# Reordering GpSimd's queue, one chunk's scores and one product in a two-layer attention kernel

## The chip, the cores and the metric

The kernel runs on one core of a Trainium2 chip. The metric is the device time of one launch in microseconds (us); the time before is the median of three runs.

## The reference

The input x holds 8 samples of 128 channels by 48 x 48 positions, float32: 2304 tokens of 128 channels each. What is computed, cut to what matters (group norm, leaky ReLU and layer norm as usual; `q`, `k`, `v` are projections of the normalized input with its position table; `_to_tokens` and `_from_tokens` only transpose):

```python
    # layer 0
    attn = jnp.einsum('bkn,bkm->bnm', q, k) / jnp.sqrt(jnp.float32(Kdim))
    attn_masked = attn * mask + (1.0 - mask) * -10000.0       # mask: lower triangle
    attn_masked = jax.nn.softmax(attn_masked, axis=-1) * mask
    x = x + jnp.einsum('bnm,bvm->bvn', attn_masked, v)
    # layer 1, on tokens
    t = _to_tokens(x)
    n = _ln_t(t)
    t = t + jnp.einsum('bnm,bmd->bnd', softmax(jnp.einsum('bnd,bmd->bnm', n, n)), n)
    # a recurrence over the 2304 tokens, with batch statistics of Wx
    t = t + _L1_ffn_ref(_ln_t(t), W, V, gamma, beta)
    x = _from_tokens(t, x)
```

In the second attention queries and keys are the same tensor, so its matrix of scores is symmetric.

## The kernel before, in words

**Tiles.** A sample's 2304 tokens are 6 chunks of 384 (`QC`), each of 3 blocks of 128. Samples, chunks and blocks are counted from 0. Partition size is 128 throughout; everything is float32. In names such as s_1_2_6, the numbers are sample, chunk and block.

**Per sample, about 204 us, there are two parts.** `Causal` does the masked attention of layer 0. For chunk j and block m up to the diagonal: scores on TensorE (PE, L1032), exponential on ScalarE (ACT, L1034), for blocks on the diagonal a multiplication with a triangle on GpSimd (POOL, L1037, the "mask"), then the product with the values on PE (L1043). VectorE (DVE) adds up the sums (L1054, L1058). When a chunk is complete, `Causal.after` starts a chain of steps: sums, residual (L1105), inverse root on POOL (`rooted`, L943), normalization on DVE (`normed`, L948). Then, for chunks 0 to 3, the normalized tokens are turned through memory; for chunks 4 and 5 `back` transposes them on PE (tile tb, L953) and ACT copies them into xh (L1129), and `shifted` adds 1 to the token-major copy xhT (POOL, L1124) and takes 1 off the residual t1t (POOL, L1125).

`Full` does the second attention. It uses the symmetry: only blocks at or right of the diagonal are scored ("direct": score L1294, exponential L1296, product L1316). The transposes of these are used for the other half. For a block of a later chunk n, DVE transposes 32 x 32 squares into a tile t (L1261); three of these fill it, `store` writes it to DRAM tile e_j_n with four DMAs of SyncE (SP, L1212), and `load` reads it back as tile g_i_j (SP, L1204; three buffers) for the "turned" products of chunk j (L1304). Blocks in a chunk's own triangle are "mirrored": DVE (L1229), out to DRAM (`out_of`, POOL, tile m, L1242), back in with four DMAs (`back_in`, POOL, tile gm, L1246), products at L1312, which are the chunk's last items. When a chunk is complete, `Full.after` starts its chain: a copy of the result (L1336), transposes (of_t, L953), residual and moments on DVE, root on POOL (L1368), a transpose of the roots (L1373), `spread` (SP: roots and turned result to DRAM, L1379, L1382), `fetch` (SP: t2x at L1386 and scale at L1388), `product` (the FFN weights times t2x on PE, tile wx, L1394; an ACT copy in `keep`; DVE at L1395 and L1396) and `stored`.

At the end comes the recurrence, which the change doesn't touch.

**What sets the order.** One list, `stream`, holds all items (one score with its product) of all samples. An item's score is issued three items ahead of its product (`LAG`). The first three items of the next sample's `Causal` are woven into the last six of a sample's stream. `Full.items()` orders a chunk's direct and turned items by a fraction, (k + 0.5) / count, for each kind. Everything else, such as the chains of the `after` methods and the next sample's projections (`project`: PE L895 and L898, tiles pj, read by DVE at L902 and L903), is issued between items by a planner, `Stream`. It keeps an estimate of the time (`now`) and of when each engine is free. A step is (function, PE cost, list of engine costs), and sets when the next step of its chain is due; a cost with an empty engine name is a plain delay. After each item `tick` runs up to two steps that are due:

```python
    def run(self, chain):
        work, cost, ops = chain.steps.popleft()
        ...
        end = self.spend(cost, chain.at) if cost else max(self.now, chain.at)
        chain.at = self.then(end, ops)
        work()
    ...
    def finish(self, chain):
        while chain.steps:
            self.run(chain)
        self.now = max(self.now, chain.at)
```

So `finish` issues all that is left of a chain at once and moves the planner's time to its end. Engines execute what is issued to them in this order; semaphores guard the data. `Full.begin` of chunk 0 finishes the chain of the chunk of `Causal` whose tokens it needs, so the transposes tb of chunk 5 are issued right ahead of the score of block 15. Prefetching g tiles (`prefetch`) is tried at every item of `Full`: loads first, then stores that are due.

Of the kernel before, what the change touches and what calls it, by code (L numbers as in the profile page):

```python
# [604 lines left out]
def fast_path(ctx: ExitStack, tc: tile.TileContext, x, pe, w_ffn, out, x_tok, w_qkv, w_pos, v_t, gamma_beta, flag):  # L605
    nc = tc.nc
# [7 lines left out]
    NQ = N // QC  # L614
# [52 lines left out]
    with ExitStack() as actx:  # L667
# [16 lines left out]
        def psum_s(name):  # L684
            return ps_s.tile([P, CH], F32, tag="s", name=name)
# [6 lines left out]
        def chunk_tile(tag, name, holder=None, steps=0, bufs=2):  # L692

            if holder is not None:
                before = holders.setdefault(tag, deque([({}, 0)] * bufs))
                old, n = before.popleft()
                before.append((holder, steps))
                if "chain" in old:
                    st.advance(old["chain"], n)
            return (work if bufs == 2 else work1).tile([P, QC], F32, tag=tag, name=name)  # L700
# [85 lines left out]
        st = Stream()  # L786
# [74 lines left out]
        def following(b, n=None):  # L861

            if n is not None:
                whole[b] = n
            n = whole.get(b, -1) + 1
            if 0 < n < NQ and n <= allowed.get(b, EARLY) and (b, n) not in projected:
                project(b, n)
# [55 lines left out]
        def bounds(b):  # L923

            qk = small2.tile([P, 2], F32, tag="qk", name=f"qk_{b}")
            nc.vector.tensor_reduce(qk, largest[b], AX.X, ALU.max)
            nc.vector.tensor_mul(bound[:, b : b + 1], qk[:, 0:1], qk[:, 1:2])
# [18 lines left out]
        def normalize(dst, y, mv, rs):  # L946
            for g in range(QB):
                nc.vector.tensor_scalar(dst[:, ts(g, P)], y[:, ts(g, P)], mv[:, g, 0:1], rs[:, g : g + 1], ALU.subtract, ALU.mult)  # L948
# [49 lines left out]
        def listed(chunks):  # L998
            return [(j, w, i == 0, i == len(ws) - 1) for j, ws in enumerate(chunks) for i, w in enumerate(ws)]

        t1_tok, x_hat, normed_chunks = {}, {}, {}

        class Causal:
# [5 lines left out]
            @staticmethod  # L1009
            def items():  # L1010

                chunks = []
                for j in range(NQ):
                    others, own = list(range(QB * j)), list(range(QB * j, QB * (j + 1)))
                    chunks.append(others[:QB] + own + others[QB:])
                return listed(chunks)
# [4 lines left out]

            def begin(self, j, m, first):
                b = self.b
                if first:
                    st.finish(projected[b, j])
                    allowed[b] = j + EARLY
                    following(b)
                    if j == NQ - 1:
                        bounds(b)
                off = self.offset(j, m)  # L1030
                s = psum_s(f"s_{b}_{j}_{m}")
                nc.tensor.matmul(s[:, off:QC], keys[b][:, ts(m, P)], queries[b, j][:, off:], start=True, stop=True)  # L1032
                p = pp.tile([P, QC], F32, tag="p", name=f"p_{b}_{j}_{m}")
                nc.scalar.activation(p[:, off:], s[:, off:QC], AF.Exp, scale=SCALE)  # L1034
                ops = [("ACT", 0.16 + (QC - off) * 0.00085)]
                if m >= QB * j:
                    nc.gpsimd.tensor_mul(p[:, off : off + P], p[:, off : off + P], triu)  # L1037
                    ops.append(("POOL", 0.5))
                return p, st.then(st.spend((QC - off) * US), ops)
# [21 lines left out]
            def after(self, j, o):  # L1061
                b = self.b
# [5 lines left out]
                if far:  # L1068
                    ot = turn_result(o, f"c_{b}_{j}", c, False)
                    at = st.then(st.now, [("DVE", 0.57)])  # L1070
                    through = token_major(c, ot, f"c_{b}_{j}", "toc", 5)
                else:
                    o_sb = chunk_tile("o", f"oc_{b}_{j}", c, 3)
                    nc.scalar.copy(by_block(o_sb), o[:, :QC].rearrange("p (a g r) -> p a g r", a=R, g=QB))
                    at = st.then(st.now, [("ACT", 0.5)])
# [38 lines left out]
                def normed():  # L1114
# [4 lines left out]
                    c["y"] = x_hat[b][0][:, QB * j : QB * (j + 1), :].rearrange("p g c -> p (g c)")  # L1119
                    normalize(c["y"], t1_tok[b, j], c["mv"], c["rs"])  # L1120

                def shifted():

                    nc.gpsimd.tensor_scalar_add(c["y"], c["y"], 1.0)  # L1124
                    nc.gpsimd.tensor_scalar_add(t1_tok[b, j], t1_tok[b, j], -1.0)  # L1125

                def back():
                    tp = transposed(c["y"], f"tb_{b}_{j}")
# [15 lines left out]
                def get():  # L1144
# [5 lines left out]
                ways = [  # L1150
                    (turn_normed, 0.0, [("DVE", 0.57)]),
                    (shifted, 0.0, [("POOL", 1.2)]),
                    (put, 0.0, [("", 4.0)]),
                    (get, 0.0, [("", 4.0)]),
# [13 lines left out]
        class Full:  # L1168
# [12 lines left out]
            @staticmethod  # L1181
            def items():
                chunks = []
                for j in range(NQ):
                    ahead = [("direct", QB * n + g) for n in range(j, NQ) for g in range(QB)]
                    turn = [("turned", i, g) for i in range(j) for g in range(QB)]
                    both = [((k + 0.5) / len(ahead), w) for k, w in enumerate(ahead)]
                    both += [((k + 0.5) / len(turn), w) for k, w in enumerate(turn)]
                    order_of = [w for _, w in sorted(both, key=lambda e: e[0])]
                    for own in ahead[QB - 2 :: -1]:  # L1190
                        order_of.remove(own)
                        order_of.insert(0, own)
                    chunks.append(order_of + [("mirrored", g) for g in range(1, QB)])
                return listed(chunks)
# [28 lines left out]
            def mirror(self, j, g, p, ready):  # L1223

                b, left = self.b, QB - 1 - g
                if g == 0:
                    self.tm = chunk_tile("tm", f"tm_{b}_{j}", bufs=1).rearrange("p (b q r) -> p b q r", b=R, q=QB)
                first = g * (QB - 1)
                nc.vector.transpose(  # L1229
                    self.tm[:, :, first : first + left, :].rearrange("p b q r -> p q b r"),  # L1230
                    p[:, (g + 1) * P :].rearrange("p (q b r) -> p q b r", q=left, b=R),
                )
                at = st.then(ready, [("DVE", 0.17 + left * 0.13)])
                if g < QB - 2:
                    return
                gm = chunk_tile("gm", f"gm_{b}_{j}", bufs=1).rearrange("p (a q r) -> p a q r", a=R, q=QB)
                self.gm = gm
                d = dpool.tile([P, R, QB * SQ], F32, tag=f"m_{j % 2}", name=f"m_{b}_{j}")
                tm = self.tm

                def out_of():
                    nc.gpsimd.dma_start(d, tm.rearrange("p b q r -> p b (q r)"))  # L1242

                def back_in():
                    for r in range(R):
                        nc.gpsimd.dma_start(  # L1246
                            gm[ts(r, SQ)].rearrange("c a q r -> c a (q r)"), d.rearrange("(a c) b f -> b c a f", a=R)[r]
                        )

                self.moved = st.add([(out_of, 0.0, [("POOL", 1.2), ("", 3.0)]), (back_in, 0.0, [("POOL", 5.0), ("", 3.0)])], at + 0.6 - st.now)  # L1250

            def turned(self, j, m, p, ready):

# [70 lines left out]
            def after(self, j, o):  # L1324
                b = self.b
# [4 lines left out]
                if far:  # L1330
                    ot = turn_result(o, f"f_{b}_{j}", c, True)
                    at = st.then(st.now, [("DVE", 0.57)])
                    through = token_major(c, ot, f"f_{b}_{j}", "tof", 3)
                else:
                    o_sb = chunk_tile("o", f"of_{b}_{j}", c, 1)
                    nc.scalar.copy(o_sb, o[:, :QC])  # L1336
                    at = st.then(st.now, [("ACT", 0.5)])
# [106 lines left out]
                if last:  # L1444
                    steps = [
                        (keep_last, 0.35, [("ACT", 0.85)]),
                        (normed, 0.0, [("DVE", 1.1)]),
                        (back, 0.35, [("ACT", 0.5)]),
                        (statistics, QC * US, [("DVE", 0.55), ("ACT", 0.85)]),
                    ]  # L1450
                else:
                    steps = [
                        (turn_root, 0.0, [("DVE", 0.15)]),
                        (spread, 0.0, [("", 13.0)]),
                        (fetch, 0.0, [("", 9.0)]),
                        (product, QC * US, [("DVE", 1.0)]),
                        (stored, 0.0, [("ACT", 0.85)]),
                    ]
# [31 lines left out]
        LAG = 3  # L1490
        stream = []
        for b in range(B):
            part, items = Causal(b), Causal.items()
            if b:

                for k in range(QB):
                    stream.insert(len(stream) - 2 * QB + k + 1, (part, *items[k]))
                items = items[QB:]
            stream += [(part, *i) for i in items]
            part = Full(b)  # L1500
            stream += [(part, *i) for i in part.items()]
        ready, o = {}, {}
        for n in range(len(stream) + LAG):
            if n < len(stream):
                part, j, what, first, last = stream[n]
# [5 lines left out]
            if n >= LAG:  # L1511
                part, j, what, first, last = stream[n - LAG]
# [200 lines left out]
```

## Time and profile before

| what | value |
|---|---|
| median of three runs | 1737.05 us (1737.0 to 1739.15) |
| the profiled run's own time | 1735.51 us |
| its span, first to last instruction | 1733.7 us |
| granted TensorE clock | 0.996 |
| score or product of 384 columns on PE (L1316, four matmuls for two) | 1.29 us for two |
| mask on POOL (L1037), mean | 471 ns |
| issue of one gm load on POOL (L1246), mean | 562 ns |
| root on POOL (L943; L1368), mean | 995 ns; 881 ns |
| shift on POOL (L1124), mean | 1296 ns |
| gm load, issue to landing, least / median / most | 2.1 / 3.3 / 6.9 us |

In the profile, a line of the timeline gives the start in us, the duration in us, the engine, the line of the kernel, the operation and its output and inputs; "x4" means four instructions one after the other, and brackets hold how long the engine had stood idle and what ended that. SPq is SyncE's queue, which issues DMAs. A line of the waits gives who waited for what, the total, the times and the longest.

### The profile page before, as it was taken

The page shows a single profiled execution, that of the slowest core. Times are in us where ns is not written, and L with a number is a line of the kernel's source. Part 1 is how long each engine was busy: PE and PEld are TensorE (multiplying, and loading weights), DVE is VectorE, ACT ScalarE, POOL GpSimd, SP SyncE. Part 2 cuts the span into 40 slices and gives each one's busy share as a digit, 9 for nine tenths or more (in the row PEclk, how much of TensorE's full clock was granted, in tenths as well). Part 3 has the DMA queues.
Part 4 walks back from the last instruction along what each step waited for, and adds up shares of the span by engine and source line. Part 5 has one row for each costly group of instructions (what it writes and reads, how often), then busy time and mean ns, then how long its engine had stood idle before and what let it go on. Part 6 is the DMA issues. An engine that isn't in the chain of part 4 may idle for free.

```text
span 1733.7 us, 22462 instructions
## 1 busy us (share of the span) xinstructions
PE 1692.1 (98%) x6243; PEld 1083.3 (62%) x6243; DVE 1205.0 (70%) x3291; ACT 684.4 (39%) x1300; POOL 445.2 (26%) x637
## 2 busy tenths in 40 slices
PE   9999999999999999999999999999999999999986
PEld 6666666666666666666666666666666666666665
DVE  5875578656886478855786567864688556884467
ACT  3344334443344423443344433443334432444345
POOL 1232122311233122321214112332213212242116
PEclk9999999999999999999999999999999999999998
DMA  3336764578445874468635675447843687247868
GB/s 121 106 89 201 229 192 114 128 204 244 135 108 143 226 237 124 88 193 236 200 105 123 188 233 151 124 121 224 254 132 78 165 233 226 64 98 200 222 235 221
DMA packets 316586, 291.13 MB, mean 168 GB/s; under 512 B 195777, under 2 KB 280674, under 8 KB 315940
## 3 DMA queue, kind: packets, MB, share of 16 engines
q1 hardware_dynamic: 306284, 267.71, 54.9%
q0 software_dynamic: 9936, 21.51, 4.5%
q8 instruction: 51, 0.84, 0.2%
q14 instruction: 83, 0.68, 0.1%
q10 hardware_dynamic: 232, 0.40, 0.1%
HBM read 163.61 MB, written 125.90 MB: 167 GB/s over the span
## 4 chain that ended last, share of the span: by engine, by line
PE 89%; DMA 5%; DVE 2%; SPq 1%; POOL 1%; issue 1%; ACT 1%; DVEq 0%; POOLq 0%; ACTq 0%
PE s L1032 17%; PE o L1043 17%; PE s L1294 15%; PE o L1316 15%; PE o L1304 11%; PE pj L895 3%; DMA g<-e 2%; DMA t2x<-t_d 2%; PE z L1626 2%; PE o L1312 2%; PE pj L898 2%; PE wx L1394 2%; SPq L1212 1%; POOL gm L1246 1%; PE of_t L953 1%
## 5 line engine op out<-in xcount | busy, mean ns | idle before, releaser
L1296 ACT ACTIVATE p<-s,shift 128x384 f32<-128x384 f32 (+2 forms) x504 | 274.8, 551 | 552.2 <-PE s L1294 482.7
L1034 ACT ACTIVATE p<-s 128x384 f32<-128x384 f32 (+2 forms) x504 | 231.1, 461 | 410.7 <-PE s L1032 359.7
L1294 PE MATMUL s<-xh 128*128 128x384 f32 (+2 forms) x1008 | 379.8, 458 | 4.5 <-ACT xh L1129 4.5
L1043 PE MATMUL o<-p,vT 128*128 128x384 f32 (+2 forms) x1008 | 377.7, 456 | 4.7 <-POOL p L1037 4.7
L1032 PE MATMUL s<-q,k 128*128 128x384 f32 (+2 forms) x1008 | 380.6, 459 | 0.1
L1316 PE MATMUL o<-p,xhT 128*128 128x384 f32 (+2 forms) x1008 | 367.6, 456 | 0.0
L1304 PE MATMUL o<-g,xhT 128*128 128x384 f32 x720 | 276.2, 487 | 6.1 <-DMA g<-e 6.1
L1261 DVE STREAM_TRANSPOSE t<-p 128x384 f32<-128x384 f32 x360 | 183.8, 549 | 139.2 <-DMA e<-t 90.3
L1316 PEld LDWEIGHTS o<-p,xhT 128*128 128x128 f32 x1008 | 189.2, 190 | 118.8 <-ACT p L1296 0.3
L1043 PEld LDWEIGHTS o<-p,vT 128*128 128x128 f32 x1008 | 186.7, 190 | 115.8 <-POOL p L1037 9.0
L1294 PEld LDWEIGHTS s<-xh 128*128 128x128 f32 x1008 | 184.2, 190 | 110.2 <-ACT xh L1129 6.5
L1032 PEld LDWEIGHTS s<-q,k 128*128 128x128 f32 x1008 | 182.3, 190 | 98.3 <-issue 2.2
L1058 DVE TENSOR_TENSOR acc<-acc,p 128x384 f32<-128x384 f32 (+2 forms) x408 | 209.2, 513 | 22.5 <-ACT p L1034 1.2
L1304 PEld LDWEIGHTS o<-g,xhT 128*128 128x128 f32 x720 | 131.5, 190 | 84.2 <-DMA g<-e 8.8
L1037 POOL TENSOR_TENSOR p<-p,triu 128x128 f32<-128x128 f32 x144 | 67.2, 471 | 437.1 <-ACT p L1034 436.9
L1246 POOL DMA_DIRECT2D gm<-m x192 | 106.9, 562 | 67.4 <-PE pj L895 30.6
L1368 POOL TENSOR_TENSOR roots<-ve_f,mhalf 128x3 f32<-128x3 f32 x48 | 42.3, 881 | 252.2 <-DVE ve_f L937 252.0
L1124 POOL TENSOR_SCALAR xhT<-xhT 128x384 f32<-128x384 f32 x48 | 62.2, 1296 | 106.7 <-DVE yt L1133 56.8
L1242 POOL DMA_DIRECT2D m<-tm x48 | 29.0, 605 | 208.3 <-DVE tm L1229 207.8
L1395 DVE TENSOR_TENSOR scale<-wx,scale 128x384 f32<-128x384 f32 x46 | 25.6, 556 | 80.2 <-PE wx L1394 72.4
L895 PE MATMUL pj<-xn,wT 128*128 128x384 f32 x192 | 77.9, 488 | 1.5 <-DVE xn L888 1.5
L902 DVE TENSOR_TENSOR q<-pj,pb 128x384 f32<-128x384 f32 x48 | 26.7, 556 | 68.9 <-PE pj L895 68.9
(250 smaller groups left out, 1695.7 us busy)
## 6 DMA issues: line engine op xcount, KB each, us to landing
e<-t SPq DMA_DIRECT2D x480, 144.0 KB
g<-e SPq DMA_DIRECT2D x120, 576.0 KB
pb<-posb_d SPq DMA_DIRECT2D x42, 576.0 KB
t1t<-in_x_tok_dram SPq DMA_DIRECT2D x48, 192.0 KB
m<-tm POOLq DMA_DIRECT2D x48, 192.0 KB, 4.4
gm<-m POOLq DMA_DIRECT2D x192, 48.0 KB, 3.3
t_d<-tt SPq DMA_DIRECT2D x184, 48.0 KB
t2x<-t_d SPq DMA_DIRECT2D x46, 192.0 KB
```

What stands on the lines that cost most here:

```text
L895: nc.tensor.matmul(ps[:, :QC], wT[:, j, :], xn, start=True, stop=True)
L1032: nc.tensor.matmul(s[:, off:QC], keys[b][:, ts(m, P)], queries[b, j][:, off:], start=True, stop=True)
L1034: nc.scalar.activation(p[:, off:], s[:, off:QC], AF.Exp, scale=SCALE)
L1037: nc.gpsimd.tensor_mul(p[:, off : off + P], p[:, off : off + P], triu)
L1043: nc.tensor.matmul(o[:, off:QC], vals[b][:, ts(m, P)], p[:, off:], start=first, stop=last)
L1058: nc.vector.tensor_add(a[:, off:], a[:, off:], p[:, off:])
L1246: nc.gpsimd.dma_start(gm[ts(r, SQ)].rearrange("c a q r -> c a (q r)"), d.rearrange("(a c) b f -> b c a f", a=R)[r])
L1261: nc.vector.transpose(t[:, :, :, g, :].rearrange("p b j r -> p j b r"), p.rearrange("p (j b r) -> p j b r", j=QB, b=R))
L1294: nc.tensor.matmul(s[:, off:QC], xh[:, ts(m, P)], xh[:, j * QC + off : (j + 1) * QC], start=True, stop=True)
L1296: nc.scalar.activation(p[:, off:], s[:, off:QC], AF.Exp, bias=shift)
L1304: nc.tensor.matmul(out_ap, xhT[:, QB * i + g, :], p, start=first, stop=last)
L1316: nc.tensor.matmul(o[:, off:QC], xhT[:, what[1], :], p[:, off:], start=first, stop=last)
```

## The change

Four edits, all to the order of issue:

- At the first item of each sample but the first, the chain that moves the previous sample's last mirrored blocks (m out, gm in) is finished (`st.finish(self.behind.moved)`). `behind` is the previous sample's `Full`.
- In `Causal.after`, the second shift (-1 on t1t) of chunk 4 becomes a step of its own, due 12 us later; for chunk 0 of `Full`, `back_in` is due 12 and not 3 us after `out_of`.
- In `Full.items()`, the places of chunk 4's direct items are multiplied by 0.6, so that they come earlier among the turned ones.
- In `Full.after`, `product` is due 12 and not 9 us after `fetch`.

```diff
@@ Causal.begin
                 b = self.b
+                if first and b and j == 0:
+                    st.finish(self.behind.moved)
                 if first:
                     st.finish(projected[b, j])
@@ Causal.after
+                def lowered():
+                    nc.gpsimd.tensor_scalar_add(t1_tok[b, j], t1_tok[b, j], -1.0)
+
                 def shifted():
 
                     nc.gpsimd.tensor_scalar_add(c["y"], c["y"], 1.0)
-                    nc.gpsimd.tensor_scalar_add(t1_tok[b, j], t1_tok[b, j], -1.0)
+                    if j == NQ - 2:
+                        st.add([(lowered, 0.0, [("POOL", 1.2)])], 12.0)
+                    else:
+                        lowered()
@@ Full.items
-                    both = [((k + 0.5) / len(ahead), w) for k, w in enumerate(ahead)]
+                    both = [((k + 0.5) / len(ahead) * (0.6 if j == NQ - 2 else 1.0), w) for k, w in enumerate(ahead)]
@@ Full.mirror
-                self.moved = st.add([(out_of, 0.0, [("POOL", 1.2), ("", 3.0)]), (back_in, 0.0, [("POOL", 5.0), ("", 3.0)])], at + 0.6 - st.now)
+                self.moved = st.add([(out_of, 0.0, [("POOL", 1.2), ("", 12.0 if j == 0 else 3.0)]), (back_in, 0.0, [("POOL", 5.0), ("", 3.0)])], at + 0.6 - st.now)
@@ Full.after
-                        (fetch, 0.0, [("", 9.0)]),
+                        (fetch, 0.0, [("", 12.0)]),
                         (product, QC * US, [("DVE", 1.0)]),
@@ the stream
         for b in range(B):
+            behind = stream[-1][0] if b else None
             part, items = Causal(b), Causal.items()
+            part.behind = behind
```

## Prediction

> **What bounds the kernel now.** I read the engines' busy time on the page first, then TensorE's waits, then the stretch of time around each kind of wait.
>
> ```profile
> PE 1692.1 (98%) x6243; PEld 1083.3 (62%) x6243; DVE 1205.0 (70%) x3291; ACT 684.4 (39%) x1300; POOL 445.2 (26%) x637
> ```
>
> PE is busy for 1692.1 of 1733.7 us, and no other engine comes near. The built programs hold the same instructions on every engine before and after; only their order differs. So PE's busy time stays, and the change can move nothing but the 41.6 us in which PE stands idle. TensorE's waits, the largest first, say what those are (line, what ended the wait: us in total, times, longest):
>
> ```profile
> PE o L1304 <- DMA g<-e: 6.1, 6, 2.4
> PE o L1043 <- POOL p L1037: 4.7, 7, 0.7
> PE s L1294 <- ACT xh L1129: 4.5, 8, 0.6
> PE wx L1394 <- DMA t2x<-t_d: 3.8, 5, 1.2
> ...
> PE o L1312 <- DMA gm<-m: 1.6, 1, 1.6
> ```
>
> The first four make 19.1 us, and come at the same place in most of the eight samples (counted from 0). The mask wait is read from GpSimd's timeline at the first change of sample (start, duration):
>
> ```profile
> 228.43 0.87 POOL L1368 TENSOR_TENSOR roots<-ve_f,mhalf 128x3 f32<-128x3 f32 x1 [6.42 <-DVE ve_f L937]
> 232.88 0.46 POOL L1037 TENSOR_TENSOR p<-p,triu 128x128 f32<-128x128 f32 x1 [3.58 <-ACT p L1034]
> 233.54 2.25 POOL L1246 DMA_DIRECT2D gm<-m  x4 [0.21 <-PE o L1304]
> 235.82 0.87 POOL L1037 TENSOR_TENSOR p<-p,triu 128x128 f32<-128x128 f32 x2
> ```
>
> The four gm loads sit between the first mask and the next two; GpSimd was idle for 3.58 us just before. PE's product at 236.34 stood 0.66 us for the second mask. The g wait is worst in sample 4, in SyncE's issues, then PE's row:
>
> ```profile
> 1034.04 0.42 SPq L1204 DMA_DIRECT2D g<-e  x1
> 1034.51 0.43 SPq L854 DMA_DIRECT2D pb<-posb_d  x1
> 1034.98 2.70 SPq L1212 DMA_DIRECT2D e<-t  x4
> 1037.90 0.65 SPq L1204 DMA_DIRECT2D g<-e  x1
> ```
> ```profile
> 1045.42 0.91 PE L1304 MATMUL o<-g,xhT 128*128 128x384 f32 x2 [0.93 <-DMA g<-e]
> ```
>
> The g load at 1037.90 is queued right after the four stores of e_4_5 and needs 7.48 us to land (the chain of waits gives that piece the same number); other g loads take 3.4 to 4.9.
>
> **What the Trainium skill says.** "TensorE: Matmul & The Clock Gate", its specification table: GpSimd's queue is strict first in, first out. The trace agrees: the second mask's scores were there, and it stood behind 2.25 us of loads. "DMA: Bandwidth & Descriptors", "Anatomy of one DMA": a GpSimd DMA takes about 2.0 us plus bytes at 436 GB/s, so an estimated 2.1 us for a 48-KB gm load. Here that is the floor only: issue to landing of the gm loads is 2.1 / 3.3 / 6.9 us (least, median, most). Same page, "Queues, rings and completion order": each DMA engine goes round its queues packet by packet, so GpSimd's loads share with SyncE's but don't stand behind its whole backlog. The trace agrees: in samples 1 to 7 the last gm load of chunk 0 landed 3.06 to 3.51 us after issue, though the DMA engines were busy 0.91 to 0.99 of that time.
>
> **The change, part by part** (against the profiled run's 1735.5 us).
>
> *Masks.* Finishing the move of the last chunk at the next sample's first item puts the four gm loads ahead of the first mask. The data they read was out at 227.6, the root before them ends at 229.30, so they run 229.3 to 231.55, before the mask at 232.88. The mask wait goes: 7 x 0.66 = 4.7 us. The loads' use (241.6) only gets safer. The price: finishing moves the planner's clock on, and so three projection blocks and the last chunk's DVE chain of 3.84 us (dn to the turned tt) are issued earlier, now ahead of the DVE read of a projection and of a running sum. Worked by hand at the first change of sample, the mask of block 7 in that sample's chunk 2 ends at 255.9 to 256.2, where PE wants it at 256.2: between 0 and about 1 us per change, 0 to 7 us in all. I take 0.15 x 7 = 1.0.
>
> *Shift and root, chunk 0's gm loads.* GpSimd now does: chunk 4's first shift, chunk 5's root, chunk 5's two shifts, the four gm loads, chunk 4's second shift. Before, it did:
>
> ```profile
> 126.67 2.26 POOL L1246 DMA_DIRECT2D gm<-m  x4
> 128.94 0.89 POOL L943 TENSOR_TENSOR rs_c<-ve_c,mhalf 128x3 f32<-128x3 f32 x1
> 132.79 1.18 POOL L1124 TENSOR_SCALAR xhT<-xhT 128x384 f32<-128x384 f32 x1 [2.96 <-PE tb L953]
> 133.94 1.17 POOL L1125 TENSOR_SCALAR t1t<-t1t 128x384 f32<-128x384 f32 x1
> ```
> ```profile
> 132.21 0.49 PE L953 MATMUL tb<-ident,xhT 128*128 128x128 f32 x3
> 133.27 0.91 PE L1294 MATMUL s<-xh 128*128 128x384 f32 x2 [0.57 <-ACT xh L1129]
> ...
> 140.25 0.38 PE L1312 MATMUL o<-gm,xhT 128*128 128x128 f32 x2
> ```
>
> The root comes 1.9 us sooner, but the transpose tb and the score that reads its copy keep their places next to each other on PE. The wait of 0.57 us is that transpose and the ACT copy, not the root: 8 x 0.57 stays. The loads get dearer: they now stand behind a shift that waits for tb. Chunk 4's second shift (1.17 us) goes behind them at no cost: its reader, chunk 4's residual, comes at 226 us. Issued at 135.1 to 136.8 instead of 126.7 to 128.4, the last has 140.25 - 136.8 = 3.46 us to land, the same in all samples, against 3.06 to 3.51 measured. In samples 1, 2 and 4 the DMA engines show 1.00 to 1.02 busy in the new stretch (343 to 352 GB/s), so slightly longer: I estimate 3.7, a stall of 0.24 x 8 = 1.9 us. From below 0 (landing 3.4 or less), from above the 5.6 of chunk 2's loads: 2.14 x 8 = 17.1.
>
> *Chunk 4's scores early.* Factor 0.6 brings blocks 14 to 17 forward among chunk 4's items, so that the e_4_5 stores are issued five places earlier, before g_2_5 and not between g_2_5 and g_3_5. The two g loads behind the stores landed in 6.0 to 7.5 us in samples 4 to 6; undisturbed 3.4 to 4.9. PE gives g_3_5 about 5.4 us (6.0 before, less wx_3's 0.65, which moves behind it), so the waits in samples 4 to 6 (0.30, 0.93, 0.35, 1.09 = 2.7) go. In the last sample the budget is 4.1 (waits of 0.98 and 2.41): 3.4 us becomes about 1.6, the middle of 0.4 to 2.8. Gain 6.1 - 1.6 = 4.5. Cover: chunk 4's own gm loads have 0.1 to 2.8 us to spare and meet the stores sooner; none is charged, up to 2 us is in the range.
>
> *Product later.* Due 12 rather than 9 us after the fetch, wx of chunk 0 goes about three items on; a score and a product are 2 x 0.645, so 3.9 us against a longest wait of 1.24. All five go: 3.8 us. What takes its place on PE are scores and products whose data is there. Other chunks' wx have 3 us or more to spare.
>
> Sum: 1735.5 - 4.7 - 3.8 - 4.5 + 1.9 + 1.0 = 1725.4. The profiled run lies 1.5 us under the median of the runs shown, 1737.05 (its span, 1733.7, 1.8 below itself), so 1.5 is put back: about 1727.
>
> **The rivals.**
> A. *Chunk 0's gm loads land late* (slower). If they behave as chunk 2's, whose last load took 4.1 to 5.7 us, the path is PE's mirrored product L1312 in each sample. At 5.6 the sum is 1727 - 1.9 + 17.1 = 1742. It passes no change where 8 x (landing - 3.46) exceeds the other net gain of 12.0, from about 4.95 us on. For it: the new stretch has a higher DMA share than chunk 2's (0.72 to 0.86). Against: the low landings above came at a share of 0.91 to 0.99.
> B. *DVE falls behind at the change of sample.* The 3.84 us chain delays sums that free p buffers; at 0.9 us x 7 = 6.3 instead of 1.0 the time is 1732. For it: DVE is at 70% and the margin is 0 to 1 us. Against: PSUM buffers in that stretch are not needed by it.
> C. *The g loads gain nothing*: the stores, moved, delay g_2_5 or the gm loads of chunk 4 instead. 4.5 less gain: 1731.5. For it: the same bytes in the same stretch; against: g_2_5 has more PE work ahead of it.
> D. *The earlier root also removes the copy's wait*: 1727 - 4.6 = 1722.5. Against: the adjacent transpose.
>
> **How the numbers follow.** Forecast 0.55 (1723 to 1731), A 0.11 (1738 to 1753), B 0.14, C 0.13, D 0.07. A difference of 0.2%, 3.5 us, is about what a measurement can tell from no change here. The forecast's and D's times are all faster than that; of B and C (0.27) about half is, and half falls within it. Faster 0.77, same 0.13, slower 0.10. The range takes in D with the costs at zero (1720) and B and C together (1737), and leaves out A.
>
> **What would show it.** Right: no wait at L1043 for a mask, none at L1394; L1304's g wait below 2 us; L1294's wait on the copy still 8 x 0.57; a new wait at L1312 for gm of about 2 us; PE busy 1692. Wrong: gm loads of chunk 0 landing in over 4.5 us, PE waiting at L1043 or L1032 on DVE or ACT after a change of sample, or g waits as before.

## The result and the profile after

No difference that can be measured: 1739.14 us median after (22 runs, 1734.65 to 1746.9) against 1740.06 before (22 runs beside them, 1733.74 to 1756.61), a ratio of 0.9997 with a 95% interval of 0.9983 to 1.0011. The forecast was 1727 us, 0.6% faster. The profiled run after took 1737.57 us, its span is 1735.8.

Here are the busy times on the page after, and TensorE's three largest waits (line, what ended the wait: us in total, times, longest). The change moved the lines: L1043 is now L1045, L1304 is L1312, L1312 is L1320, L1394 is L1402, and the score that waits for the copy, L1294, is L1302.

```profile
PE 1693.6 (98%) x6243; PEld 1084.6 (62%) x6243; DVE 1204.3 (69%) x3291; ACT 681.4 (39%) x1300; POOL 458.7 (26%) x637
```
```profile
PE o L1320 <- DMA gm<-m: 9.5, 9, 1.9
PE o L1312 <- DMA g<-e: 7.4, 10, 1.3
PE s L1302 <- ACT xh L1137: 4.5, 8, 0.6
```

The waits for masks and for t2x, 8.5 us together, are gone to the last one. But gm is now waited for during 9.5 us instead of 1.6, and g during 7.4 instead of 6.1. PE is idle (span less busy time) for 42.2 us against 41.6. So the change took away the two waits that it was aimed at, and nearly the same time came back at gm and g.

The mask's stretch is as forecast. GpSimd's timeline at the first change of sample (start, duration):

```profile
230.25 0.87 POOL L1376 TENSOR_TENSOR roots<-ve_f,mhalf 128x3 f32<-128x3 f32 x1 [7.86 <-DVE ve_f L937]
231.09 2.23 POOL L1254 DMA_DIRECT2D gm<-m  x4
234.28 0.45 POOL L1039 TENSOR_TENSOR p<-p,triu 128x128 f32<-128x128 f32 x1 [0.96 <-ACT p L1036]
```

The loads run between root and first mask, and the mask waits only for its exponential. Chunk 0's gm loads, in the first sample, are at the place that was forecast, to 0.1 us:

```profile
132.84 1.18 POOL L1129 TENSOR_SCALAR xhT<-xhT 128x384 f32<-128x384 f32 x1 [4.80 <-PE tb L953]
133.98 1.18 POOL L1125 TENSOR_SCALAR t1t<-t1t 128x384 f32<-128x384 f32 x1
135.10 2.28 POOL L1254 DMA_DIRECT2D gm<-m  x4
```
```profile
141.37 0.46 PE L1320 MATMUL o<-gm,xhT 128*128 128x128 f32 x2 [0.90 <-DMA gm<-m]
```

They landed later than forecast, and PE stood for 0.90 us. Over the eight samples the last of the four loads takes 4.2 us on average from issue to landing (3.1 to 4.9), against 3.3 before.

Counted through in PE's order, six of the nine gm waits are chunk 0's (5.8 us) and three are chunk 4's (3.7). Of the ten g waits, five are for g_2_5, in samples 1, 2, 4, 5 and 6 (5.3 us), four of 0.2 us are for g_3_5, and one of 1.2 is in the last sample. This is a wait for g_2_5 in sample 1, on SyncE, then on PE:

```profile
421.05 0.34 SPq L1212 DMA_DIRECT2D g<-e  x1
421.49 1.98 SPq L1220 DMA_DIRECT2D e<-t  x4
423.65 0.59 SPq L1394 DMA_DIRECT2D t2x<-t_d  x1
424.53 0.45 SPq L1396 DMA_DIRECT2D scale<-rs  x1
425.03 0.44 SPq L1212 DMA_DIRECT2D g<-e  x1
```
```profile
432.20 1.56 PE L1312 MATMUL o<-g,xhT 128*128 128x384 f32 x4 [1.03 <-DMA g<-e]
```

The load of g_2_5 (425.03) now stands behind the four stores and behind chunk 3's fetch (t2x and scale). PE asks for it at 431.17, 6.1 us after its issue.

### The profile page after: what moved, and what is told of

Its sections match the earlier page's. It is cut to its first block, busy times and chain, and to the rows that moved or that the text cites. A ratio compares the mean times of both kernels' runs of the same rounds, so it can differ in the third digit from the quotient of the medians.

```text
span 1735.8 us, 22434 instructions
## 1 busy us (share of the span) xinstructions
PE 1693.6 (98%) x6243; PEld 1084.6 (62%) x6243; DVE 1204.3 (69%) x3291; ACT 681.4 (39%) x1300; POOL 458.7 (26%) x637
## 4 chain that ended last, share of the span: by engine, by line
PE 87%; DMA 6%; DVE 3%; issue 2%; POOL 2%; ACT 0%; POOLq 0%; SPq 0%; DVEq 0%; ACTq 0%
PE s L1034 17%; PE o L1045 17%; PE s L1302 14%; PE o L1324 14%; PE o L1312 11%; PE pj L895 3%; DMA g<-e 2%; DMA gm<-m 2%; PE o L1320 2%; PE z L1636 2%; PE wx L1402 2%; PE pj L898 1%; DMA m<-tm 1%; POOL gm L1254 1%; PE of_t L953 1%
## 5 line engine op out<-in xcount | busy, mean ns | idle before, releaser
L1304 ACT ACTIVATE p<-s,shift 128x384 f32<-128x384 f32 (+2 forms) x504 | 274.5, 550 | 579.4 <-PE s L1302 521.9
L1302 PE MATMUL s<-xh 128*128 128x384 f32 (+2 forms) x1008 | 379.8, 458 | 4.5 <-ACT xh L1137 4.5
L1045 PE MATMUL o<-p,vT 128*128 128x384 f32 (+2 forms) x1008 | 377.0, 456 | 0.0
L1312 PE MATMUL o<-g,xhT 128*128 128x384 f32 x720 | 282.4, 488 | 7.4 <-DMA g<-e 7.4
L1045 PEld LDWEIGHTS o<-p,vT 128*128 128x128 f32 x1008 | 187.2, 190 | 108.8 <-POOL p L1039 1.6
L1302 PEld LDWEIGHTS s<-xh 128*128 128x128 f32 x1008 | 183.6, 190 | 107.9 <-ACT xh L1137 6.5
L1312 PEld LDWEIGHTS o<-g,xhT 128*128 128x128 f32 x720 | 131.3, 190 | 85.8 <-DMA g<-e 12.2
L1039 POOL TENSOR_TENSOR p<-p,triu 128x128 f32<-128x128 f32 x144 | 77.8, 542 | 339.4 <-ACT p L1036 339.4
L943 POOL TENSOR_TENSOR rs_c<-ve_c,mhalf 128x3 f32<-128x3 f32 x48 | 45.6, 950 | 157.4 <-DVE ve_c L937 157.4
```

The costliest lines, as they stand in the source:

```text
L1045: nc.tensor.matmul(o[:, off:QC], vals[b][:, ts(m, P)], p[:, off:], start=first, stop=last)
L1302: nc.tensor.matmul(s[:, off:QC], xh[:, ts(m, P)], xh[:, j * QC + off : (j + 1) * QC], start=True, stop=True)
L1304: nc.scalar.activation(p[:, off:], s[:, off:QC], AF.Exp, bias=shift)
L1312: nc.tensor.matmul(out_ap, xhT[:, QB * i + g, :], p, start=first, stop=last)
```

## The experiments

In all of them I read three things. The first is the ratio to the kernel before, run beside it on the same chip. The second is PE's idle time in the profile, which leaves out how fast the matmuls themselves ran (PE's busy time differs by up to 12 us between these profiles, for the same instructions). The third is which waits the idle time is made of: for a mask, for t2x, gm and g, and for the copy into xh. Waits for DMAs also change where an edit doesn't touch them: those for t2x were 3.8 us before, 2.0 in moved_only and 1.8 in late_loads_only. Each kernel has one profile, so how much of this is the new order and how much would differ between two executions of one kernel is not shown.

| kernel | ratio, 95% interval | PE idle | mask | t2x | gm | g | copy |
|---|---|---|---|---|---|---|---|
| before | 1 | 41.6 | 4.7 | 3.8 | 1.6 | 6.1 | 4.5 |
| full change | 0.9997 (0.9983 to 1.0011) | 42.2 | 0 | 0 | 9.5 | 7.4 | 4.5 |
| moved_only | 0.9951 (0.9933 to 0.9969) | 34.0 | 0 | 2.0 | 0 | 6.3 | 4.5 |
| late_loads_only | 1.0046 (1.0027 to 1.0065) | 47.5 | 4.7 | 1.8 | 8.9 | 7.2 | 4.5 |
| early_scores_only | 0.9997 (0.9980 to 1.0014) | 45.7 | 9.1 | 1.3 | 0.7 | 5.0 | 4.5 |
| product_only | 0.9935 (0.9910 to 0.9960) | 34.4 | 0 | 0 | 0.7 | 8.3 | 4.5 |
| without_late_loads | 0.9936 (0.9916 to 0.9957) | 36.4 | 0 | 0 | 3.4 | 5.5 | 4.5 |
| without_early_scores | 1.0037 (1.0018 to 1.0055) | 48.2 | 9.2 | 0 | 6.1 | 7.3 | 4.5 |
| without_product | 1.0056 (1.0039 to 1.0074) | 49.1 | 0 | 1.7 | 15.0 | 2.9 | 4.5 |
| moved_product | 1.0004 (0.9989 to 1.0018) | 43.1 | 8.9 | 0 | 2.6 | 6.3 | 4.5 |
| loads_ahead | 0.9981 (0.9968 to 0.9993) | 40.7 | 0 | 0 | 8.6 | 5.9 | 4.5 |
| stores_held | 1.0024 (1.0008 to 1.0040) | 50.0 | 0 | 0 | 11.8 | 11.8 | 4.5 |
| moved_product_m | 0.9983 (0.9970 to 0.9996) | 41.7 | 7.9 | 0 | 1.9 | 6.5 | 4.5 |
| moved_product_tm | 0.9948 (0.9928 to 0.9967) | 34.7 | 0 | 0 | 3.5 | 5.5 | 4.5 |
| moved_product_m_tb | 0.9934 (0.9914 to 0.9953) | 36.6 | 6.8 | 0 | 0 | 7.8 | 0 |
| moved_product_tm_tb | 0.9951 (0.9936 to 0.9967) | 33.8 | 0 | 0 | 1.0 | 4.7 | 0 |
| moved_tb | 0.9944 (0.9929 to 0.9960) | 34.3 | 0 | 2.8 | 0.5 | 8.8 | 0 |
| without_late_loads_tb | 0.9913 (0.9898 to 0.9928) | 31.6 | 0 | 0 | 2.3 | 6.7 | 0 |

(All waits in us; less than 0.5 is written 0.)

The two measures don't always agree. For seven of the seventeen kernels the difference in idle time lies outside the interval of the difference in time. In early_scores_only idle grows by 4.1 us, while the time changes by -3.5 to +2.4; in without_late_loads_tb idle falls by 10.0 us, the time by 12.5 to 17.8. An idle figure holds for its one profile; whether a kernel is faster is told by the ratio.

**One edit at a time.** Each of the four alone, on the kernel before; the diffs are those of the change.

> Only the first edit: the previous sample's last gm loads are issued at the next sample's first item. Theory (the four edits act one by one, gains eaten by two new waits): the seven mask waits of 0.66 us go, nothing else changes: 4.7 us less, PE's g, gm, copy and wx waits as before (6.1, 1.6, 4.5, 3.8). Rival (a gain is caught up by the next wait): the mask waits go, but PE waits elsewhere for 3 us or more longer than before (g loads or DVE after the change of sample), and the time stays within 1 us.

> Only the second edit: chunk 4's second shift on its own and chunk 0's gm loads due 12 us after m. Theory: chunk 0's gm loads are issued 8.4 us later, behind chunk 5's shifts, and land some 4.2 us later than that on average; PE waits at the mirrored product 0.7 us per sample, 5 to 7 us in all, and the kernel is slower by that. Rival (the late landing comes from traffic that the other edits moved): waits of 0 to 2 us in all, time within 2 us of before.

> Only the third edit: chunk 4's direct items earlier. Theory: the stores of e_4_5, moved ahead of g_2_5, shift the g wait from g_3_5 to g_2_5 and make it longer (7 to 8 us in all against 6.1), and chunk 4's gm loads, beside the same stores, are waited for longer (3 to 4 us against 1.6): 2 to 4 us slower. Rival (those waits come with the product's later place or the moved loads): g waits below 3 us, 3 to 4 us faster.

> Only the fourth edit: the product due 12 and not 9 us after the fetch. Theory: all five waits for t2x go, 3.8 us less, other waits as before. Rival: PE waits as long elsewhere (g loads behind the moved fetches), no gain.

The first edit alone and the fourth alone are each worth some 7 us of PE's idle time. The second costs 5.9, and the third 4.1 in its profile (in its time no cost shows). (Of the first's 7.6, 4.7 are the masks; the rest is t2x and chunk 4's gm, DMA waits that the edit doesn't touch.) The second does what the theory says: chunk 0's late loads make 7.8 us of its 8.9 us of gm waits, in seven of eight samples (the rest is chunk 4's in one). The third does not: the waits for g and gm don't grow. But the mask waits nearly double, from 0.66 to 1.25 us or more each, since GpSimd now does a root between the first mask and the loads, and waits for projections (pj) grow from 1.5 to 3.9 us. And the fourth takes the mask waits away too, which I hadn't expected: it moves m and with it the loads, to behind the second mask. So the first and the fourth edit both claim the same 4.7 us, and the four don't add: alone they sum to -4.8 us, together they make +0.6.

**Undoing one edit at a time.** Again with the diffs of the change, one left out; and the two good ones alone.

> The first and the fourth edit alone (moved gm loads, product later). In the runs of one edit each, either of the two took the mask waits away, so their gains do not add. Theory: no mask wait, no t2x wait; g waits of 6 to 8 us and the copy's 4.5 us stay; PE idle (span less busy time) 32 to 34 us against 41.6 before: 8 to 9 us faster than before, and so faster than the full change. Rival (the two gains are used up by g loads once PE runs ahead): g waits of 12 us or more, no more than 4 us faster.

> The full change without its second edit: chunk 0's gm loads are issued 3 us after m again. Theory: only the waits for chunk 0's gm (5.8 us in the profile of the full change) go; chunk 4's gm waits and the g waits stay (3.7 and 7.4): PE idle about 36 us, 6 us faster than the full change. Rival (the DMA traffic just moves the wait to the g loads): PE idle 40 us or more.

> The full change without its third edit: chunk 4's direct items where they were. Theory: chunk 0's gm waits stay (5 to 7 us), chunk 4's gm waits fall to 0 to 1.7 us, the g waits move back from g_2_5 to g_3_5 and are 6 to 8 us: PE idle 38 to 40 us, 2 to 4 faster than the full change. Rival (the forecast was right on the stores, and the g waits of the full change have another cause): g waits rise above 9 us, PE idle as in the full change or more.

Leaving out the second edit gives 5.8 us of idle time back, just what chunk 0's loads cost, and 0.6% of the time. Chunk 4's gm waits stay near the full change's; the g waits are 1.9 us shorter, and a wait of 2.0 us for the next sample's group norm has come in:

```profile
PE o L1309 <- DMA g<-e: 5.5, 9, 1.2
PE s L1299 <- ACT xh L1134: 4.5, 8, 0.6
PE o L1317 <- DMA gm<-m: 3.4, 2, 1.9
```

Leaving out the third, which alone costs 4.1 us of idle time, makes the kernel slower instead, and the two edits that gain 7 us each alone gain nothing together. Both theories missed here: the mask waits are back, at 8.9 and 9.2 us. GpSimd's timeline of moved_product shows why, then DVE's two transposes that fill tm, then PE:

```profile
226.33 0.87 POOL L1373 TENSOR_TENSOR roots<-ve_f,mhalf 128x3 f32<-128x3 f32 x1 [12.26 <-DVE ve_f L937]
227.26 0.61 POOL L1247 DMA_DIRECT2D m<-tm  x1
232.89 2.18 POOL L1251 DMA_DIRECT2D gm<-m  x4 [5.02 <-PE s L1034]
235.09 0.87 POOL L1039 TENSOR_TENSOR p<-p,triu 128x128 f32<-128x128 f32 x2
```
```profile
221.52 0.43 DVE L1234 STREAM_TRANSPOSE tm<-p 128x256 f32<-128x256 f32 x1
226.69 0.27 DVE L1234 STREAM_TRANSPOSE tm<-p 128x128 f32<-128x128 f32 x1
```
```profile
235.61 0.91 PE L1045 MATMUL o<-p,vT 128*128 128x384 f32 x2 [1.93 <-POOL p L1039]
```

m goes out at 227.3 and not at 221.4, and lands at 232.3. The four loads, now ahead of the first mask by the first edit, wait for it, and the mask behind them comes 1.9 us late. (The releaser in brackets, a score on PE, had long been done; the landing of m is what came last.) I first took the root ahead of m for the cause:

```diff
-                self.moved = st.add([(out_of, ...), (back_in, ...)], at + 0.6 - st.now)
+                self.moved = st.add([(out_of, ...), (back_in, ...)], 0.0 if j == NQ - 1 else at + 0.6 - st.now)
```

> The first and fourth edit, and chunk 5's m goes out as soon as planned, which puts its issue ahead of chunk 4's root on GpSimd. With the two edits alone it stood behind that root, which waits for DVE, and so the moved gm loads and the masks behind them were late (8.9 us of mask waits). Theory: m is issued at about 221 and not 227 us, the gm loads run before the first mask, the mask waits go (0 to 1 us left): PE idle 33 to 36 us against 43.1. Rival (the moved loads are late for another reason, as the landing of m): mask waits of 4 us or more stay.

That theory fell: m is now ahead of the root, but issued at 227.5 all the same, and mask waits of 7.9 us stay. What m waits for is the second transpose of tm, 5.2 us after the first: between them DVE does chunk 4's residual and moments, which the planner issues there once the fourth edit is in. So I put that chain off:

```diff
-                ], max(at, st.free["DVE"]) + 0.2 - st.now)
+                ], max(at, st.free["DVE"]) + (0.2 if j != NQ - 2 else 3.0) - st.now)
```

> The first and fourth edit, and chunk 4's chain of Full starts 2.8 us later in the plan, so that on DVE both transposes tm of chunk 5 stand ahead of its residual and moments. Theory: m is issued at about 221 instead of 227 us, the mask waits (8.9 us with the two edits alone) fall below 1 us; g waits of 6 to 8 us stay: PE idle 33 to 36 us. Rival (m lands late whenever it is issued): mask waits of 4 us or more.

The second transpose follows the first by 1.4 us, m goes out at 223.2, the loads run well ahead of the mask at 231.5, and no mask is waited for:

```profile
222.63 0.30 DVE L1234 STREAM_TRANSPOSE tm<-p 128x128 f32<-128x128 f32 x1
```
```profile
223.23 0.56 POOL L1247 DMA_DIRECT2D m<-tm  x1 [9.81 <-DVE tm L1234]
226.16 2.17 POOL L1251 DMA_DIRECT2D gm<-m  x4 [2.37 <-DMA m<-tm]
231.49 0.45 POOL L1039 TENSOR_TENSOR p<-p,triu 128x128 f32<-128x128 f32 x1 [3.16 <-ACT p L1036]
```

So the third edit's use in the full change lies where I didn't look: it keeps m and the residual chain in their old order, which the fourth edit upsets. DVE in the full change (dn is the first step of the residual chain):

```profile
221.23 0.31 DVE L1237 STREAM_TRANSPOSE tm<-p 128x128 f32<-128x128 f32 x1 [0.96 <-ACT p L1304]
226.83 0.55 DVE L1354 TENSOR_REDUCE dn<-of_t 128x3 f32<-128x384 f32 x1
```

**Chunk 0's loads.** The full change, with the loads ahead of chunk 5's second shift:

```diff
-                    if j == NQ - 2:
+                    if j >= NQ - 2:
                         st.add([(lowered, 0.0, [("POOL", 1.2)])], 12.0)
```

> The full change, but chunk 5's second shift too is put off behind chunk 0's gm loads, so that these are issued 1.17 us sooner. Theory (PE waits because the loads are issued late and take as long as the traffic of that stretch makes them, 3.1 to 4.9 us): the waits for chunk 0's gm fall from 5.8 us to 0 to 1.5 us in all, PE idle about 37 us. Rival (they land when the stores of that stretch are through, whenever they were issued): the landing moves by less than 0.4 us and 4 us of waits or more stay.

The rival's numbers held; its reason, the stores of that stretch, is not shown. Issued earlier, the last load takes 5.2 us on average instead of 4.2. Of the 1.17 us hardly anything arrives, and chunk 0's waits fall only from 5.8 to 4.3 us. The DMA engines are somewhat fuller in the new stretch. From first issue to landing, their busy share in samples 1 to 7 is 0.81 to 0.93 in the kernel before, 0.91 to 0.96 after and 0.92 to 0.99 in loads_ahead. Sample 4 in each of the three, in that order (window, its length; busy time of PE, PEld, DVE, ACT, POOL; clock, DMA share, GB/s):

```profile
942.10:947.00 4.90, 4.76 (x17) 2.67 (x15) 3.44 (x10) 2.38 (x5) 3.18 (x7) 1.00 0.90 268
```
```profile
952.00:958.10 6.10, 5.37 (x18) 2.98 (x16) 4.74 (x11) 2.21 (x4) 3.43 (x6) 1.00 0.96 299
```
```profile
951.30:958.40 7.10, 6.51 (x21) 3.61 (x19) 5.77 (x14) 2.80 (x5) 4.58 (x7) 1.00 0.98 292
```

But the share does not tell when a load lands. Inside the full change it is 0.95 in sample 6, where the last load took 3.1 us, and 0.91 in sample 7, where it took 4.2. And counted from the last issue on, as the prediction counted it, the full change is no fuller (0.92 to 0.98) than the kernel before (0.91 to 0.99).

**The g wait.** Two kernels. In the first the stores of e_4_5 wait in the plan until g_2_5 has been issued; in the second the product is due after 9 us again:

```diff
-                while self.to_store and self.to_store[0][3] <= st.now:
+                while self.to_store and self.to_store[0][3] <= st.now and (self.to_store[0][:2] != (NQ - 2, NQ - 1) or (2, NQ - 1) in self.loaded):
```

> The full change, but the stores of e_4_5 are held until g_2_5 has been issued, so that they stand behind it again as in the kernel before. Theory (the stores ahead of it make g_2_5 land about 1 us late): the waits for g_2_5 in samples 1, 2, 4, 5 and 6 (5.3 us) go and at most 2 to 3 us come at g_3_5; chunk 0's gm waits (5.8) stay: PE idle 37 to 40 us against 42.2. Rival (the whole stretch is short of DMA time, whatever the order): g waits of 6 us or more in all, only at other tiles, PE idle above 41.

> The full change without its fourth edit: the product due 9 us after the fetch again. Theory (the later product took wx of chunk 3 and a projection out of the time between the issue and the use of g_2_5, which shrank from about 8.8 us to 6): with the stores ahead of it still, g_2_5 is not waited for in samples 0 to 6 (less than 0.5 us in all); waits for t2x of 1 to 4 us and chunk 0's gm waits (5 to 7) stay. Rival (the stores alone delay it): waits for g_2_5 of 4 us or more.

Holding the stores was a miss for the theory. g_2_5 is waited for during 1.1 us, in one sample. But g_3_5, which PE asks for about 5.4 us after its issue and which has the stores ahead of it, is waited for during 10.8 us in six samples. That makes 11.8 us of g waits in all, more than in either kernel. So the stores, wherever they go, fall on the load behind them, and of the two places the one ahead of g_2_5 is better. without_product shows the other half. With the stores ahead of g_2_5 as in the full change, PE asks for it 8.8 us after its issue instead of about 6, and no g_2_5 is waited for:

```profile
PE o L1320 <- DMA gm<-m: 15.0, 9, 2.1
...
PE pj L895 <- DVE xn L888: 3.9, 9, 0.9
PE o L1312 <- DMA g<-e: 2.9, 2, 1.7
...
PE wx L1402 <- DMA t2x<-t_d: 1.7, 3, 0.8
```

The third edit alone, early_scores_only, shows the same 8.8 us and no wait for g_2_5. So it takes both edits to make g_2_5 late. The expectation's reason, wx of chunk 3, is not it: that product comes after g_2_5's use in both kernels (in sample 1 of the full change at 437.6 us, the use at 432.2). The traces show two other reasons.

The larger one is in SyncE's queue. A g load can go out when PE has done the last product from the buffer that it will fill. In without_product g_2_5 goes out 0.03 us after that in samples 0 to 6. In the full change it goes out 1.4 to 1.7 us after (in sample 1 the buffer is free at 423.5), because the load of chunk 3's scale stands ahead of it and waits in turn: scale has one buffer, and ACT has to copy chunk 2's scale out of it first. The later product has put that copy off. This is the copy in the full change, which ends at 424.51, just ahead of scale's issue at 424.53 in SyncE's lines further up; then SyncE in without_product, where the fetch comes behind g_2_5:

```profile
423.39 1.12 ACT L1408 COPY wx<-scale 128x384 f32<-128x384 f32 x1
```
```profile
430.20 0.48 SPq L1212 DMA_DIRECT2D g<-e  x1
430.78 0.40 SPq L1394 DMA_DIRECT2D t2x<-t_d  x1
431.27 0.38 SPq L1396 DMA_DIRECT2D scale<-rs  x1
```

The smaller reason is PE's work. From the free buffer to the moment when PE asks for g_2_5 it is 7.65 us in the full change (8.80 in without_product), since two projections are done before the buffer comes free and not after. In stores_held g_2_5 goes out late too, by 1.4 us behind the same load of scale, but without stores ahead, and costs 1.1 us. So the stores alone cost g_2_5 nothing, the late issue alone 1.1 us, and the two together 5.3. No run took the fetch out of g_2_5's way.

As a whole without_product is the slowest kernel of all: chunk 0's loads alone make 14.2 us of its gm waits, with landings of 5.3 us on average. Why they land another 1.1 us later there than in the full change is open; no run was made for it.

**The copy's wait.** In four kernels chunk 5's transposes tb are issued one item earlier, so that a score and a product stand between them and the score that reads their copy (the line moves the other chunks' chains by one item, too):

```diff
-                    st.finish(normed_chunks[b, what[1] // QB])
+                    st.finish(normed_chunks[b, min(what[1] + 1, NB - 1) // QB])
```

> As moved_product_m, and chunk 5's transposes tb are issued one item earlier, with a score and a product between them and the score that reads their copy. Theory (the 0.57 us is transpose and copy, not the root, as the forecast had it): the eight waits for the copy, 4.5 us, fall below 1 us, and nothing takes their place: PE idle 29 to 31 us. Rival (the normalization on DVE, behind the root, ends too late for that): PE waits as long for DVE at the transposes, idle as in moved_product_m.

> The full change without its second edit, and chunk 5's transposes tb one item earlier. Theory: the copy's 4.5 us go here too: PE idle 36.4 less 4.5, some 32 us; against the kernel before about 9 to 10 us. Rival: the wait moves to the transposes, idle stays at 36.

> As moved_product_tm, and chunk 5's transposes tb one item earlier, which took the copy's wait of 4.5 us away in two runs. Theory: PE idle 29 to 31 us, ratio about 0.993 or less. Rival: a wait elsewhere comes in its place, idle 33 us or more.

> The first edit alone and the transposes tb one item earlier. Theory: 34.0 us of PE idle with the first edit alone, less the copy's 4.5: 29 to 30 us. Rival: other waits grow by 2 us or more.

The eight waits are gone in all four, with the root where it was. What that is worth differs. In without_late_loads_tb idle falls from 36.4 to 31.6 us, all of it, and in moved_product_m_tb from 41.7 to 36.6. In moved_tb it doesn't fall (34.0 to 34.3), because waits for g and t2x grow by 3.3 us. In moved_product_tm_tb it falls by 0.9 us alone (34.7 to 33.8), because a wait for DVE ahead of the next sample's group norm (gn_m, L809) takes 6.2 us. In both the rival held. The mask waits of moved_product_m stay in its tb form too. without_late_loads_tb has the lowest ratio found, 0.9913 (0.9898 to 0.9928), though the intervals of several other kernels reach into its own. Its largest waits:

```profile
PE o L1309 <- DMA g<-e: 6.7, 12, 1.1
PE pw L1662 <- DVE off L1657: 2.6, 1, 2.6
PE o L1317 <- DMA gm<-m: 2.3, 1, 2.3
```

## Why the prediction was wrong

The steps of its sum, against the profile of the full change (us):

| step | forecast | measured |
|---|---|---|
| masks | -4.7 | -4.7 |
| DVE and planner at the change of sample | +1.0 | 0: no wait at scores or products there |
| product later (t2x) | -3.8 | -3.8 |
| copy's wait stays at 4.5 | 0 | 0 |
| chunk 0's gm loads late | +1.9 | +5.8 |
| chunk 4's gm loads, uncharged | 0 | +2.1 (1.6 to 3.7) |
| g loads | -4.5 | +1.3 (6.1 to 7.4) |
| PE busy, taken as unchanged | 0 | +1.5 |
| sum | -10.1 | +2.2 |

1735.5 and 2.2 make 1737.7 us, and the profiled run took 1737.6.

*Masks and product: right.* Both waits went, by the mechanism forecast. Not seen was that neither needs the other edits, that both edits clear the masks, and that the two alone bring the masks back.

*Chunk 0's gm loads: the path was right, the size wrong.* The term "I estimate 3.7, a stall of 0.24 x 8 = 1.9 us" failed: the last load took 4.2 us on average, PE asked for it 3.5 to 3.7 us after its issue (forecast: 3.46), and 5.8 us were waited for. The estimate rested on landings of 3.06 to 3.51 us "though the DMA engines were busy 0.91 to 0.99 of that time", and the same share was held against rival A. That share does not tell the landing: in the same part of the stretch it was 0.92 to 0.98 in the full change, and landings went up to 4.9 us. Nor does the landing move along with the issue: loads_ahead issued the loads 1.17 us sooner, and they took 1.0 us longer. Rival A named this path; its 5.6 us and 17.1 us are nearly what without_product shows (5.3 and 14.2). What makes the loads late is open.

*The g loads: wrong.* "PE gives g_3_5 about 5.4 us [...], so the waits in samples 4 to 6 [...] go" came true in its number, with 0.6 us of 2.7 left, but in part by luck: PE stood for g_2_5 first, and so asked for g_3_5 only 6.4 to 6.9 us after its issue, and was still 0.2 us too early each time. The step that failed is that the gain was counted for the load that the stores leave, and nothing was charged for the one that they now stand ahead of. g_2_5 got 5.3 us of waits. Rival C names it ("the stores, moved, delay g_2_5"); the prediction held against it that "g_2_5 has more PE work ahead of it". That was read from the kernel before. In the full change the later product takes some of that time away: 8.8 us between issue and use without it, about 6 with it. The product was priced for its own wait alone, and not for the copy of scale that it puts off and the loads that stand behind that copy on SyncE.

*Chunk 4's gm loads.* Left uncharged with up to 2 us in the range; 2.1 came. In the single edit that moves the stores they didn't grow (0.7), so they are not shown to be the stores' doing, and their waits differ between kernels from 0 (moved_only) to 4.4 us (loads_ahead).

*The busy time* lay between 1687.5 us (at a granted clock of 0.997) and 1699.2 us (at 0.991) in 18 profiles of the same instructions, so 1.5 us says nothing about the change.

*Copy's wait: right, and so was turning down rival D.* Moving tb takes the wait away with the root in its old place; the earlier root, which the full change has (127.16 instead of 128.94), did not.

*Rival B* did not come, but something of its kind did elsewhere: DVE's residual chain ahead of a transpose costs 8.9 us in moved_product, and the third edit is what keeps it away in the full change.

Behind the miss on the g loads, and behind the mask waits of moved_product, is one way of working: each edit was priced almost alone against the profile before, and the prices were added. The runs of one edit sum to -4.8 us of idle time, the full change shows +0.6, and leaving out the third edit, which alone gains nothing, makes the kernel slower.

## What to carry to other kernels

Where a planner issues instructions into queues that run in order, the price of an edit depends on the other edits: look at the program as finally ordered for what each queue holds ahead of a waiting instruction. Work out the time between a load's issue and its use there, for the load that loses time as well as for the one that gains it, and ask what the issue itself waits for. Slack that an edit spends (here 7 to 9 us of chunk 0's gm) has to buy something that the engine which sets the time (here PE) was waiting for; here the earlier root bought nothing. A load moved into another stretch is to be given a landing measured in that very stretch: an equal busy share of the DMA engines does not promise an equal landing, and an issue sooner by one us need not bring it sooner.

## What the runs showed of the hardware

GpSimd's four gm loads of chunk 0, 48 KB each, landed 3.1 to 3.5 us after the last issue in their old place, 3.1 to 4.9 in the new one, and 4.6 to 5.8 where they were issued 1.17 us sooner in that place: the landing hardly moved. The DMA engines' busy share did not tell these apart: from the last issue on it was 0.91 to 0.99 in the old place and 0.92 to 0.98 in the new one.

The Trainium skill ("DMA: Bandwidth & Descriptors", "Queues, rings and completion order") says that each DMA engine goes round its queues packet by packet; the forecast took from it that a load on GpSimd's queue does not stand behind SyncE's whole backlog. Part of the delay comes before a load's first packet: on the mean of eight samples the first packet of the four loads began 1.9 us after the first issue in the kernel before, 2.2 in the full change and 2.7 in loads_ahead. Whether the loads wait for their descriptors or for the engines no run separates, so no run here shows the page's rule or speaks against it. One mark is left untested: over chunk 0's loads in all 18 traces, that first packet came 1.3 to 2.1 us after the first issue (median 1.3) in the 63 cases in which no packet of 4608 bytes, the size in a g load, was moving meanwhile, and 1.7 to 3.4 us (median 2.1) in the 81 cases in which one was.
